# A state-space scan at the head of an eight-block kernel: weights by a second DMA queue, and half of the preparation moved into the scan

## The chip, the cores and the metric

The kernel runs on one core of a Trainium2 chip. A core has TensorE (PE, with its weight loads shown apart as PEld), VectorE (DVE), ScalarE (ACT), GpSimd (POOL) and SyncE (SP). The metric is the time on the device in microseconds (us); less is better. The time before is 2128.78 us, the median of three runs (2113.94, 2128.78 and 2228.47).

## The reference

The program sends 2048 tokens of width 128 (8 sequences of 256) through eight blocks, each as x = layernorm(x + block(x)): a state-space scan, a mixture of 8 experts, an attention with latent queries, a mixture of 64 experts, a gated linear attention, a mixture of 160 experts, six layers of linear attention, and a softmax attention. Only the first block is touched:

```python
def _L0_attn_ref(tokens, norm_w, a, b, c, skip, w_out, b_out):
    ms = jnp.mean(jnp.square(tokens), axis=-1, keepdims=True)
    x = tokens * jax.lax.rsqrt(ms + EPS) * norm_w
    x = x.reshape(B, T, H, D)                 # 8, 256, 16, 8
    a_t = jnp.tanh(a)                         # 16, 64, 64
    state0 = jnp.zeros((B, H, S), dtype=tokens.dtype)
    def step(state, x_t):
        state = jnp.tanh(jnp.einsum('bhs,hst->bht', state, a_t)
                         + jnp.einsum('bhd,hds->bhs', x_t, b))
        mixed = jnp.einsum('bhs,hsd->bhd', state, c) + skip[None] * x_t
        return (state, mixed)
    xs = jnp.moveaxis(x, 1, 0)
    _, outs = jax.lax.scan(step, state0, xs)
    outs = jnp.moveaxis(outs, 0, 1).reshape(B, T, DIM)
    return tokens + outs @ w_out.T + b_out
```

The 256 steps of the scan depend on each other; the 8 sequences and 16 heads do not.

## The kernel before

The program is straight-line code without loops at run time. A framework traces it and then orders the instructions of each engine by a simulated timeline (`schedule_with_timeline_sim=True`): the program's order is the priority, and an instruction whose operands are there in the simulation may be put ahead of one that still waits. On the chip each engine then runs its instructions in that fixed order. `behind(...)` adds an order by hand; in the scan `in_turn` gives TensorE's instructions exactly the program's order.

The 2048 tokens are held as four groups x[g] (g = 0 to 3) of 128 partitions x 4 blocks x 128 features. Group g holds sequences 2g and 2g+1; block j = 2h + m is half m of sequence 2g + h, so that half m = 0 is the first 128 tokens of a sequence. Four DMAs on SyncE's queue load them (L1269); the helper `load` (L60 to L64) puts every other load on SyncE's queue too. Its order is: the four x, three routers, `upper`, `tile_at`, two bias rows, five shared experts' weights, then in `l0_attn` (from L157) L0_a, L0_b, L0_c, L0_norm_w, L0_norm_d, L0_skip, L0_w_outT and the row L0_b_out. L0_a and L0_b have 512 KB each.

`l0_attn` prepares the scan's input group by group. POOL squares the group (L194), VectorE adds up each token's squares (L196), `inv_sqrt` takes 11 small VectorE operations (L91 to L102), four VectorE operations scale the tokens into `xs` (L200), and TensorE transposes the four blocks into one PSUM bank (`transpose4`, L128). From the bank ScalarE writes `xd` in eight operations per group (L207): the features times a column of L0_norm_d, of which a head keeps only its own features. VectorE writes `xnT` (L211), the normed input for the skip term. `xd` has the layout token pair, parity u, head-in-pair e, sequence. ScalarE also takes the tanh of L0_a (L180).

Then the scan runs in blocks of TB = 16 steps. For every eight steps, 16 products of L0_b with `xd` (L224, `inputs`) are put into two PSUM banks ahead of their use; the first of them come before the first step. A step has eight products of L0_a with the last state (L297), four for each half h of the heads, and one ScalarE tanh for each half (L306). While a half waits for its tanh, TensorE runs the other half's products, and between them two of `inputs`; after every fourth step four products of L0_c (L250, `outputs`) of the block before. When these are done, VectorE adds the skip term (L262, L263). Step 0 needs the input products of the first eight tokens of all sequences. After the scan, L336 (`xb` = 2x + b_out), the output projection (L342), L349 and a layernorm close the block, and the experts follow. L336 has no operand from the scan.

Of the kernel before, what the change touches and what calls it, by code (L numbers as in the profile page):

```python
# [10 lines left out]
F32 = mybir.dt.float32  # L11
I32 = mybir.dt.int32
U32 = mybir.dt.uint32
AF = mybir.ActivationFunctionType
ALU = mybir.AluOpType
AX = mybir.AxisListType

P = 128
B, T, D = 8, 256, 128
NT = B * T  # L20
NG = 4
# [21 lines left out]
def tile_post_ln_blocks(ctx: ExitStack, tc: tile.TileContext, I, out: bass.AP):  # L43
    nc = tc.nc
    V, S, G, PE = nc.vector, nc.scalar, nc.gpsimd, nc.tensor

    const = ctx.enter_context(tc.tile_pool(name="const", bufs=1))
    lanes = [Lane(tc, ctx, i) for i in range(2)]

    norms = [ctx.enter_context(tc.tile_pool(name=f"norm{g}", bufs=2)) for g in range(NG)]  # L50
    xs = [ctx.enter_context(tc.tile_pool(name=f"xs{g}", bufs=2)) for g in range(NG)]
    dram = ctx.enter_context(tc.tile_pool(name="dram", bufs=1, space=bass.MemoryType.DRAM))

    def bank(pool):
        return pool.tile([P, 512], F32, tag=pool.name, name=pool.name)

    def quarters(t):
        return t.rearrange("p (a b) -> p a b", b=P)

    def load(pool, key, tag=None):  # L60
        ap = I[key]
        t = pool.tile(list(ap.shape), F32, tag=tag or key, name=tag or key)
        nc.sync.dma_start(out=t, in_=ap)
        return t  # L64

    def load_row(pool, key):
# [5 lines left out]
    ident = const.tile([P, P], F32, tag="ident", name="ident")  # L72
# [10 lines left out]
    def inv_sqrt(pool, var, n, eps, scale=1.0):  # L83

        def t(tag, dt=F32):
            return pool.tile([P, n], dt, tag=f"{tag}{n}", name=tag)

        v, i, y, a, b = t("rs_v"), t("rs_i", U32), t("rs_y"), t("rs_a"), t("rs_b")  # L90
        V.tensor_scalar(v, var, scale, eps, ALU.mult, ALU.add)  # L91
        V.tensor_scalar(i, v.bitcast(U32), 1, 0xFFFFFFFF, ALU.logical_shift_right, ALU.bitwise_xor)
        V.tensor_tensor(i, i, magic[:, :n], ALU.add)
        g = i.bitcast(F32)
        V.tensor_tensor(a, g, g, ALU.mult)
        V.scalar_tensor_tensor(a, a, -1.0, v, ALU.mult, ALU.mult)
        V.tensor_scalar(b, a, 0.375, 0.875, ALU.mult, ALU.add)
        V.scalar_tensor_tensor(b, a, 1.0, b, ALU.add, ALU.mult)
        V.scalar_tensor_tensor(y, b, 1.0, g, ALU.add, ALU.mult)
        V.tensor_tensor(a, y, y, ALU.mult)  # L100
        V.scalar_tensor_tensor(a, a, -0.5, v, ALU.mult, ALU.mult)
        V.scalar_tensor_tensor(y, a, 1.5, y, ALU.add, ALU.mult)  # L102
        return y
# [20 lines left out]
    def transpose4(src, pool):  # L124

        ps = quarters(bank(pool))
        for j in range(4):
            PE.transpose(ps[:, j, :], src[:, j, :], ident)  # L128
        return ps


    x, xT = [None] * NG, [None] * NG
# [26 lines left out]
    def l0_attn(x):  # L159
# [6 lines left out]
        TB = 16  # L166
        cols = [slice(32 * c, 32 * c + 32) for c in range(4)]
        sides = [slice(0, 64), slice(64, 128)]
        with ExitStack() as es:
            wp = es.enter_context(tc.tile_pool(name="l0w", bufs=1))  # L170
            wk = es.enter_context(tc.tile_pool(name="l0k", bufs=2))
            a_sb = load(wp, "L0_a")
            b_sb = load(wp, "L0_b")
            c_sb = load(wp, "L0_c")
            normw = load(wp, "L0_norm_w")
            normd = load(wp, "L0_norm_d")
            skip = load(wp, "L0_skip")
            woT = load(wp, "L0_w_outT")
            bout = load_row(wp, "L0_b_out")
# [2 lines left out]
            xnT = wp.tile([P, T // 2, 2, B], F32, tag="xnT", name="xnT")  # L182
# [3 lines left out]
            for h in range(2):  # L186
                states.append([])
                for k in range(2):
                    t = wp.tile([P, TB * 4 * 32 + 8], F32, tag=f"st{h}{k}", name=f"st{h}{k}")
                    (V if h else G).memset(t, 0.0)  # L190
                    states[h].append(t)
            for g in range(NG):
                sq = wk.tile([P, 4, D], F32, tag="sq", name="sq")
                G.tensor_tensor(out=sq, in0=x[g], in1=x[g], op=ALU.mult)  # L194
                ms = lanes[g % 2].small.tile([P, 4], F32, tag="ms", name="ms")
                V.tensor_reduce(ms, sq, AX.X, ALU.add)  # L196
                r = inv_sqrt(norms[g], ms, 4, 1e-4, 1.0 / D)
                xs = wk.tile([P, 4, D], F32, tag="xs", name="xs")
                for j in range(4):
                    V.tensor_scalar(xs[:, j, :], x[g][:, j, :], r[:, j : j + 1], None, ALU.mult)  # L200
                ps = transpose4(xs, lanes[g % 2].ps)
                for h in range(2):
                    i = 2 * g + h
                    src = ps[:, 2 * h : 2 * h + 2, :].rearrange("p a (b u) -> p (a b) u", u=2)
                    for u in range(2):
                        for e in range(2):
                            S.activation(  # L207
                                xd[:, :, u, e, i], src[:, :, u], AF.Copy,
                                scale=normd[:, 2 * u + e : 2 * u + e + 1],
                            )  # L210
                    V.tensor_scalar(xnT[:, :, :, i], src, normw, None, ALU.mult)  # L211

            ps_m = es.enter_context(tc.tile_pool(name="ps_s", bufs=4, space=bass.MemoryType.PSUM))
            HB = TB // 2
# [69 lines left out]
            prev = [states[h][1][:, (TB - 1) * 128 :] for h in range(2)]  # L284
            for n in range(T):
                t, blk = n % TB, n // TB
                if t == 0 and blk:
                    outs, finish = outputs(blk - 1)
                if n % HB == 0:
                    now, ins = us, []  # L290
                    if n + HB < T:
                        us, ins = inputs(n + HB)
                for h in range(2):
                    for s in range(2):
                        for c in range(2):
                            k = 2 * s + c
                            in_turn(PE.matmul(  # L297
                                now[h][sides[c], n % HB // 2, n % 2, s].rearrange("p e f b -> p (e f b)"),
                                lhsT=a_sb[:, n % 2, 4 * h + k, :],
                                rhs=prev[h][:, 32 * k + 8 * (1 - c) : 32 * k + 8 * (1 - c) + 32],  # L300
                                start=False,
                                stop=(n % HB == HB - 1),
                                skip_group_check=True,
                            ))
                    st = states[h][blk % 2]
                    made_by = S.activation(  # L306
                        st[:, t * 128 : t * 128 + 128].rearrange("p (k e z b) -> p k e z b", k=4, e=2, z=2)[:, :, :, 1],
                        now[h][:, n % HB // 2, n % 2].rearrange("p s e f b -> p (s e) f b"),
                        AF.Tanh,
                    ).ins  # L310
                    if t == 0 and blk > 1:
                        tc.add_manual_dep(
                            made_by, ended[h][blk - 2].name,
                            mybir.DependencyInfo(mybir.DependencyClass.Sync, mybir.DependencyReason.DATA),
                            reason="the buffer's last block is done",
                        )
                    if t == TB - 1:
                        ended[h].append(made_by)
                    prev[h] = st[:, t * 128 : t * 128 + 136]
                    if h == 0:  # L320
                        more, ins = ins[:2], ins[2:]
                    else:
                        more, outs = (outs[:4], outs[4:]) if n % 4 == 3 else ([], outs)
                    for f in more:
                        in_turn(f())
                    if finish and not outs:
                        finish()
                        finish = None
# [129 lines left out]
    def behind(ins, other, why):  # L458

        tc.add_manual_dep(  # L460
            ins, other.name, mybir.DependencyInfo(mybir.DependencyClass.NoSync, mybir.DependencyReason.DATA), reason=why
        )
# [790 lines left out]
    with ExitStack() as moe:  # L1253
# [10 lines left out]
        x0 = []  # L1264
        with ExitStack() as es:
            xp = es.enter_context(tc.tile_pool(name="x0", bufs=NG))
            for g in range(NG):
                x0.append(xp.tile([P, 4, D], F32, tag="x0", name="x0"))
                nc.sync.dma_start(  # L1269
                    out=x0[g], in_=I["x"][g * GT : (g + 1) * GT, :].rearrange("(j p) d -> p j d", p=P)  # L1270
                )
            router0, router1, router2 = (load(mw, k) for k in ("F0_router", "F1_gate_w", "F2_router"))
            upper, tile_at = load(mw, "upper"), load(mw, "tile_at")
            bias1, bias2 = load_row(mw, "F1_gate_bias"), load_row(mw, "F2_bias")
            shared1 = tuple(load(mw, k) for k in ("F1_sg", "F1_su", "F1_sd"))
            shared2 = load(mw, "F2_sg"), load(mw, "F2_sd")
            zero = mw.tile([P, D], F32, tag="zero", name="zero")
            V.memset(zero, 0.0)
            l0_attn(x0)


        placed = [dram.tile([places, D], F32, tag=f"placed{h}", name=f"placed{h}") for h in range(2)]
# [175 lines left out]
```

## Time and profile before

| what | us |
|---|---|
| median of three runs | 2128.78 |
| lowest and highest of the three | 2113.94 and 2228.47 |
| the profiled execution's own time | 2114.01 |
| its span on the core | 2112.3 |
| preparation, up to the scan's first product (L224) | 27.03 |
| scan, up to its last step's tanh | 27.0 to 241.8 |
| PE busy over the span | 1815.5 (86%) |
| DVE, ACT, POOL busy | 1271.0, 875.4, 460.5 |
| mean granted clock of TensorE | 0.898 of full speed |

Busy time is given for each engine over the whole span; PE's is modelled, because products overlap. In a timeline row the columns are the start, the time that it covers, the engine, the line, the operation with what it writes and reads, how many instructions are merged into the row, and in brackets how long the engine had been idle and what it waited for. SPq and ACTq stand for the issue of DMAs on a queue. A row of the chain of waits has start, length, and what held the work in that time. A row of the stretches has the busy time of each engine (with the count of instructions), the granted clock, the share of the 16 DMA engines that was busy, and GB/s.

### The profile page before, as it was taken

The numbers are of one execution on the slowest core, as the hardware profiler recorded it, in microseconds if no ns is written. First come the engines' busy times: TensorE is split into PE (matmuls) and PEld (weight loads), VectorE is DVE, ScalarE is ACT, GpSimd is POOL, SyncE is SP. The second block draws the span as 40 slices with busy tenths as digits, with TensorE's granted clock in tenths as the row PEclk, the third lists the DMA queues.
The fourth block names the chain that finished last, engine by engine and source line by source line (L and its number), as shares of the span: only waits on it lengthen the run. The fifth ranks groups of instructions, "written<-read, shape, count | busy, mean of one in ns | idle before, by whom it ended". The sixth has DMA issues, their size and how long they took to land.

```text
span 2112.3 us, 38809 instructions
## 1 busy us (share of the span) xinstructions
PE 1815.5 (86%) x14138; PEld 1212.1 (57%) x14138; DVE 1271.0 (60%) x4476; ACT 875.4 (41%) x1877; POOL 460.5 (22%) x1042
## 2 busy tenths in 40 slices
PE   5999889878999999998987664679677999998797
PEld 4888645464555446544775553556455676665564
DVE  4000346867878557895559312565677998566754
ACT  4555435624754267423322111224334554434414
POOL 1000000000000000048812888850586000000000
PEclk9999989988999999998778666799888999989958
DMA  3000178403324422353147897776110000000000
GB/s 95 4 4 4 32 231 247 130 1 80 83 73 119 130 83 64 86 136 86 35 147 243 254 278 226 232 230 198 58 32 27 1 1 1 1 6 6 0 1 11
DMA packets 163455, 194.01 MB, mean 92 GB/s; under 512 B 21664, under 2 KB 117408, under 8 KB 163264
## 3 DMA queue, kind: packets, MB, share of 16 engines
q1 hardware_dynamic: 144704, 155.86, 25.5%
q0 software_dynamic: 8192, 16.79, 2.6%
q10 hardware_dynamic: 10368, 18.88, 2.4%
q8 instruction: 112, 1.84, 0.3%
q14 instruction: 79, 0.65, 0.1%
HBM read 143.68 MB, written 47.78 MB: 91 GB/s over the span
## 4 chain that ended last, share of the span: by engine, by line
PE 60%; DVE 12%; POOL 11%; DMA 7%; ACT 4%; issue 4%; SPq 2%; ACTq 0%; DVEq 0%; POOLq 0%
PE ps_s L297 7%; PE ps_o L363 6%; PE ps_m L368 6%; POOL idle L467 5%; PE ps L128 4%; PE ps_m L373 4%; POOL placed L549 4%; PE ps L1076 3%; PE ps L1070 3%; DMA w<-in_F_w_dram 3%; PE ps_o L647 3%; POOL got L658 2%; PE ps_s L224 2%; DMA got<-made,pl 2%; PE ps L1180 2%
## 5 line engine op out<-in xcount | busy, mean ns | idle before, releaser
L549 POOL DMA_INDIRECT placed<-x,pl x128 | 132.9, 1038 | 1022.5 <-DVE junk L570 915.6
L370 ACT ACTIVATE h<-ps_m 128x512 f32<-128x512 f32 x196 | 116.1, 597 | 236.8 <-PE ps_m L368 215.7
L363 PE MATMUL ps_o<-h,wd 128*128 128x512 f32 x384 | 200.8, 607 | 7.3 <-DVE h L376 7.3
L368 PE MATMUL ps_m<-xT,wg 128*128 128x512 f32 x384 | 197.7, 598 | 4.8 <-ACT h L370 4.8
L467 POOL MEMSET idle<- 128x176 f32 x768 | 192.2, 250 | 29.7
L297 PE MATMUL ps_s<-st,L_a 128*64 128x32 f32 x4096 | 192.2, 223 | 1.0
L297 PEld LDWEIGHTS ps_s<-st,L_a 128*64 128x64 f32 x4096 | 160.0, 137 | 29.6 <-ACT st L306 12.7
L376 DVE TENSOR_TENSOR h<-h,bc 128x512 f32<-128x512 f32 x192 | 131.5, 687 | 48.9 <-ACT h L370 40.2
L306 ACT ACTIVATE st<-ps_s 128x64 f32<-128x64 f32 x512 | 114.8, 224 | 99.5 <-PE ps_s L297 70.4
L658 POOL DMA_INDIRECT got<-made,pl x128 | 123.2, 962 | 111.7 <-DVE rs_v L91 86.0
L373 PE MATMUL ps_m<-xT,wu 128*128 128x512 f32 x256 | 133.9, 605 | 4.5 <-ACT h L370 3.5
L647 PE MATMUL ps_o<-w,xg 64*64 64x128 f32 x1152 | 102.5, 331 | 39.0 <-DVE xg L642 38.9
L636 PE MATMUL ps_m<-xg,w 128*64 128x64 f32 x1152 | 86.6, 266 | 54.8 <-DMA w<-in_F_w_dram 32.4
L262 DVE SCALAR_TENSOR_TENSOR outsT<-xnT,L_skip,ps 128x64 f32<-128x64 f32 x32 | 10.4, 324 | 197.4 <-PE ps L250 197.4
L363 PEld LDWEIGHTS ps_o<-h,wd 128*128 128x128 f32 x384 | 73.2, 194 | 95.8 <-issue 67.9
L368 PEld LDWEIGHTS ps_m<-xT,wg 128*128 128x128 f32 x384 | 71.2, 191 | 87.7 <-issue 65.7
L374 DVE TENSOR_TENSOR h<-h,ps_m 128x512 f32<-128x512 f32 x132 | 90.0, 682 | 44.6 <-PE ps_m L373 40.8
L636 PEld LDWEIGHTS ps_m<-xg,w 128*64 128x64 f32 x1152 | 64.1, 166 | 88.8 <-issue 33.1
L649 ACT COPY ob<-ps_o 128x512 f32<-128x512 f32 x72 | 42.1, 585 | 169.4 <-PE ps_o L647 134.0
L647 PEld LDWEIGHTS ps_o<-w,xg 64*64 64x64 f32 x1152 | 80.5, 165 | 53.9 <-DVE xg L642 46.5
L1070 PE MATMUL ps<-nT,A_w 128*128 128x512 f32 x192 | 100.3, 641 | 8.9 <-ACT nT L996 5.2
L1076 PE MATMUL ps<-A_w,hT 128*128 128x128 f32 x768 | 99.2, 282 | 7.4 <-DVE hT L1072 7.4
(357 smaller groups left out, 3718.9 us busy)
## 6 DMA issues: line engine op xcount, KB each, us to landing
bc<-comb SPq DMA_DIRECT2D x128, 256.0 KB
w<-in_F_w_dram SPq DMA_DIRECT2D x256, 96.0 KB
placed<-zero SPq DMA_DIRECT2D x72, 256.0 KB
xb<-placed SPq DMA_DIRECT2D x72, 256.0 KB
made<-ob ACTq DMA_DIRECT2D x72, 256.0 KB
w<-in_F_wg_dram SPq DMA_DIRECT2D x40, 256.0 KB
w<-in_F_wd_dram SPq DMA_DIRECT2D x40, 256.0 KB
bc<-comb SPq DMA_DIRECT2D x16, 512.0 KB
```

Source lines behind the costliest of these rows:

```text
L297: in_turn(PE.matmul(now[h][sides[c], n % HB // 2, n % 2, s].rearrange("p e f b -> p (e f b)"), lhsT=a_sb[:, n % 2, 4 * h + k, :], rhs=prev ...
L363: PE.matmul(acc[g], lhsT=w, rhs=h, start=begin, stop=end, skip_group_check=True)
L368: PE.matmul(pg, lhsT=wg, rhs=xT[g], start=True, stop=True)
L373: PE.matmul(pu, lhsT=wu, rhs=xT[g], start=True, stop=True)
L376: V.tensor_tensor(h, h, bc[:, i * GT : (i + 1) * GT], ALU.mult)
L467: after, last = G.memset(idle, 0.0).ins, after
L549: i = G.indirect_dma_start(placed[h][:, :], bass.IndirectOffsetOnAxis(rw[:, j, c : c + 1], 0), x[g][:, j, :], None).ins
L636: PE.matmul(pt[i % 2 * n : (i % 2 + 1) * n, i // 2, :], lhsT=wg[:, i, :n], rhs=xg[:, i * n : (i + 1) * n], start=True, stop=True,)
L647: PE.matmul(po[k, i // 2, :], lhsT=h[k, i // 2, :], rhs=wd[i], start=True, stop=True)
L658: i = G.indirect_dma_start(got[:, c, :], None, made[g // 2][:, :], bass.IndirectOffsetOnAxis(row[g][:, j, c : c + 1], 0)).ins
L1070: PE.matmul(ph, lhsT=w1[:, f * P : (f + 1) * P], rhs=nT, start=True, stop=True)
L1076: PE.matmul(po[:, j, :], lhsT=hT[:, f, j * P : (j + 1) * P], rhs=w2[:, f, :], start=(f == 0), stop=(f == 3),)
```

## The change

The helper `load` gets an argument for the issuing engine. L0_norm_d, L0_b and L0_a are issued by ScalarE, in this order and ahead of all other work of `l0_attn`; the other loads of the block stay on SyncE, and those of routers, biases and shared experts now follow the block in the program. `zero` is set by POOL and no longer by VectorE.

The preparation goes by halves of the sequences and no longer by groups. For half 0, ScalarE squares and adds up eight blocks (Square with an accumulator), one `inv_sqrt` works on eight columns, eight `xs` operations and eight transposes fill two banks, and `xd` is written in eight operations of 128x256, four on ScalarE and four on VectorE; `xnT` takes four of 128x256 behind them. For half 1 (`scaled(1)`), VectorE squares, sums and scales behind half 0's last `xd` operation. Its eight transposes stand in the scan, one in each of the steps 24 to 31, in TensorE's written order; after the fourth and the eighth, VectorE writes `xd` and `xnT`.

```diff
-    def load(pool, key, tag=None):
+    def load(pool, key, tag=None, by=None):
...
-        nc.sync.dma_start(out=t, in_=ap)
+        (by or nc.sync).dma_start(out=t, in_=ap)
...
-            a_sb = load(wp, "L0_a")
-            b_sb = load(wp, "L0_b")
+            normd = load(wp, "L0_norm_d", by=S)
+            b_sb = load(wp, "L0_b", by=S)
+            a_sb = load(wp, "L0_a", by=S)
+            normw = load(wp, "L0_norm_w")
             c_sb = load(wp, "L0_c")
-            normw = load(wp, "L0_norm_w")
-            normd = load(wp, "L0_norm_d")
...
-            for g in range(NG):
-                sq = wk.tile([P, 4, D], F32, tag="sq", name="sq")
-                G.tensor_tensor(out=sq, in0=x[g], in1=x[g], op=ALU.mult)
...
+            def scaled(m):
+                ms = wk.tile([P, NG, 2], F32, tag="ms", name="ms")
+                sq = wk.tile([P, D], F32, tag="sq1", name="sq")
+                for g in range(NG):
+                    for h in range(2):
+                        xj = x[g][:, 2 * h + m, :]
+                        if m == 0:
+                            S.activation(sq, xj, AF.Square, accum_out=ms[:, g, h : h + 1])
+                        else:
+                            i = V.scalar_tensor_tensor(
+                                sq, xj, 1.0, xj, ALU.mult, ALU.mult, accum_out=ms[:, g, h : h + 1]
+                            ).ins
+                            behind(i, spread[-1], "the first half of the tokens goes ahead")
+                r = inv_sqrt(wk, ms.rearrange("p g h -> p (g h)"), 2 * NG, 1e-4, 1.0 / D)
+                xs = wk.tile([P, 2 * NG, D], F32, tag="xs", name="xs")
+                for i in range(2 * NG):
+                    V.tensor_scalar(xs[:, i, :], x[i // 2][:, 2 * (i % 2) + m, :], r[:, i : i + 1], None, ALU.mult)
+                return xs
+
+            def spread_out(m, k, ps, fast):
+                ts, bs = slice(m * P // 2, (m + 1) * P // 2), slice(4 * k, 4 * k + 4)
+                src = ps.rearrange("p i (b u) -> p b u i", u=2)
+                for u in range(2):
+                    for e in range(2):
+                        scale, to = normd[:, 2 * u + e : 2 * u + e + 1], xd[:, ts, u, e, bs]
+                        if fast and e == 0:
+                            S.activation(to, src[:, :, u, :], AF.Copy, scale=scale)
+                        else:
+                            spread.append(V.tensor_scalar(to, src[:, :, u, :], scale, None, ALU.mult).ins)
+
+            def scan_norm(m, k, ps):
+                ts, bs = slice(m * P // 2, (m + 1) * P // 2), slice(4 * k, 4 * k + 4)
+                src = ps.rearrange("p i (b u) -> p b u i", u=2)
+                for u in range(2):
+                    V.tensor_scalar(xnT[:, ts, u, bs], src[:, :, u, :], normw, None, ALU.mult)
+
+            early = scaled(0)
+            halves = [transpose4(early[:, 4 * k : 4 * k + 4, :], lanes[k].ps) for k in range(2)]
+            for k in range(2):
+                spread_out(0, k, halves[k], True)
+            for k in range(2):
+                scan_norm(0, k, halves[k])
+            later = scaled(1)
...
             for n in range(T):
                 t, blk = n % TB, n // TB
+                if TB + 8 <= n < TB + 16:
+                    k, i = (n - TB - 8) // 4, n % 4
+                    if i == 0:
+                        halves[k] = quarters(bank(lanes[k].ps))
+                    in_turn(PE.transpose(halves[k][:, i, :], later[:, 4 * k + i, :], ident))
+                    if i == 3:
+                        spread_out(1, k, halves[k], False)
+                        scan_norm(1, k, halves[k])
...
+            zero = mw.tile([P, D], F32, tag="zero", name="zero")
+            G.memset(zero, 0.0)
+            l0_attn(x0)
             router0, router1, router2 = (load(mw, k) for k in ("F0_router", "F1_gate_w", "F2_router"))
...
-            zero = mw.tile([P, D], F32, tag="zero", name="zero")
-            V.memset(zero, 0.0)
-            l0_attn(x0)
```

## The prediction

> **What bounds the kernel now.** I read four views: the stretches table, the chain of waits over the first 75 us, the timeline of the same stretch, and the groups of instructions by line. The stretches come first, since they say how much there is to win.
>
> ```profile
> core 0: us, PE busy (x) PEld busy (x) DVE busy (x) ACT busy (x) POOL busy (x), PEclk, DMA share, GB/s
> 0.00:27.00 27.00, 4.69 (x16) 2.86 (x16) 20.47 (x83) 10.99 (x33) 8.47 (x13) 1.00 0.60 181
> 27.00:245.00 218.00, 215.50 (x5642) 183.73 (x5643) 18.16 (x65) 115.27 (x514) 0.00 (x0) 1.00 0.01 3
> 245.00:2112.00 1867.00, 1595.27 (x8482) 1025.51 (x8480) 1232.38 (x4328) 749.17 (x1331) 452.04 (x1029) 0.88 0.34 101
> ```
>
> TensorE does nothing but 16 transposes in the first 27 us, which is the preparation; then it is full for 218 us, which is the scan; the other 1867 us are seven further blocks, which the diff does not touch. So the front can give at most 27 us of 2112 (1.3%), and only as much of it as the scan starts earlier. The timeline says what the 27 us go into.
>
> ```profile
> 8.24 0.43 SPq L63 DMA_DIRECT2D F_sg<-in_F_sg_dram  x1
> ...
> 9.32 0.57 SPq L63 DMA_DIRECT2D L_a<-in_L_a_dram  x1
> ...
> 13.09 1.06 ACT L180 ACTIVATE L_a<-L_a 128x1024 f32<-128x1024 f32 x1 [11.06 <-DMA L_a<-in_L_a_dram]
> ...
> 15.72 2.29 ACT L207 ACTIVATE xd<-ps,L_norm_d 128x128 f32<-128x128 f32 x8 [1.58 <-DMA L_norm_d<-in_L_norm_d_dram]
> ...
> 16.80 0.69 DVE L336 SCALAR_TENSOR_TENSOR xb<-x,L_b_out 128x512 f32<-128x512 f32 x1 [1.91 <-DMA L_b_out<-in_L_b_out_dram]
> ...
> 18.98 3.32 ACT L207 ACTIVATE xd<-ps,L_norm_d 128x128 f32<-128x128 f32 x12 [0.97 <-DVE rs_y L99]
> ...
> 25.54 0.68 DVE L211 TENSOR_SCALAR xnT<-ps,L_norm_w 128x256 f32<-128x256 f32 x1 [0.34 <-ACT xd L207]
> 26.25 1.25 ACT L207 ACTIVATE xd<-ps,L_norm_d 128x128 f32<-128x128 f32 x4 [0.74 <-DVE xnT L211]
> 27.03 1.79 PEld L224 LDWEIGHTS ps_s<-xd,L_b 128*64 128x64 f32 x32 [4.20 <-ACT xd L207]
> 27.03 1.98 PE L224 MATMUL ps_s<-xd,L_b 128*64 128x64 f32 x32 [3.89 <-ACT xd L207]
> ```
>
> Two things are to be seen. First, the weights come late: SyncE's queue sends the routers and shared experts first, L_a goes out at 9.32, L_norm_d lands at 15.7, and the planner put L336, work for after the scan, where VectorE waits 1.91 us for L_b_out. Second, from 15.7 to 27.0 ScalarE and VectorE pass each PSUM bank back and forth (xd 32 x 0.286 us, xnT 8 x 0.685 us), and the scan's first product waits for the last xd. The chain of waits has the input's own part:
>
> ```profile
> 2.35 4.55 DMA x<-in_x_dram
> 6.92 0.33 SPq L63
> ...
> 27.03 1.98 PE ps_s L224 x32
> ```
>
> The last quarter of x is there at 6.9, and some load behind it on SyncE's queue waits for it. The scan is a tight loop:
>
> ```profile
> 35.90 0.66 PE L297 MATMUL ps_s<-st,L_a 128*64 128x32 f32 x16
> 36.36 0.20 PEld L224 LDWEIGHTS ps_s<-xd,L_b 128*64 128x64 f32 x4
> 36.37 0.46 ACT L306 ACTIVATE st<-ps_s 128x64 f32<-128x64 f32 x2 [0.29 <-PE ps_s L297]
> ```
>
> One step is 0.75 us (35.90 to 36.65); weight loads alone fill 0.55 + 0.20 of it, so what is put between steps on TensorE is paid.
>
> **The change, part by part.** All times are in the profiled execution: span 2112.3, time 2114.0.
>
> (1) x, a, b. L_norm_d, L_b and L_a (1 MB) are issued by ScalarE, beside the four x (1 MB) on SyncE. If the two don't disturb each other, the last x lands at 6.9 as now. If they share, 2 MB at the 318 GB/s of the stretch from 12 to 16 us, where the DMA engines were 93% busy with one queue, take 6.6 us from 2.4: 9.0. I take 9.0, the row with nearly full engines; ends 6.9 and 9.5. [...]
>
> (2) Sum of squares. POOL's 4 x 1.03 us and four reductions of 0.68 us go; in come 8 ACT Square of 128x128 with an accumulator. ACT on 128x128 costs 0.286 (2.29/8), the accumulator read 0.199 (row of L1032): 0.49 each, two per x, so 0.97 after the last x: 10.0. The Tanh of L_a (1.06 us) stands ahead of them in the program. If the planner leaves it last, 10.0; between the second and third x, 9.0 + 1.06 + 4 x 0.49 = 12.0; ahead of all, 14.0. I take 11.0, because the small x are ready before the 512 KB of L_a. ScalarE's three issues of 0.45 to 0.57 us end by 3.7 and hide behind the x.
>
> (3) inv_sqrt, once for 8 columns where there were four interleaved: 11 small operations, 0.2 us from start to start when in a row (249.04 to 250.63 holds nine): 2.2 us, 13.2. L336's two xb (0.69 each) may again be put among them, and L_b_out, now the ninth or tenth transfer, may come as late as 12; nothing to 3 us, I take 1.0: 14.2.
>
> (4) xs and transposes. Eight xs at 0.215 (0.86/4): 15.9; four transposes of the second bank at 0.28 (2.25/8): 17.0. The first bank hides under the xs.
>
> (5) Spread. 8 of 128x256, ACT and DVE alternating on each bank, second bank last: 2 x 0.384 (L641) + 2 x between 0.42 (L1016, 128x256 from PSUM) and 0.685 (L211, strided output): 1.6 to 2.1. I take 1.9, near L211, whose scattered output it resembles: 18.9. The norm for the skip term (4 x 0.685) follows behind, and has until the first block's outputs, after step 16. So the scan's first product starts at 19.0 for 27.0: **8.0 us won.**
>
> (6) The second half. `later` (8 DVE squares of some 0.46 (0.378 + 0.081, L570), 2.2 + 1.7) needs 7.6 us behind the 2.7 of (5), so it ends near 29; step 24 comes at about 40. This cover is 11 us; without it TensorE would wait. Eight transposes stand in TensorE's written order, one a step: 0.21 (two L342 within the scan moved it 0.42 us, 230.84 to 231.26) to 0.28 each, 1.7 to 2.2, and 0 if a step had slack. I take **2.0 us lost**. The 12 DVE operations behind them (12 x 0.685 = 8.2 us) are needed by step 120, 70 us later: nothing, as DVE is 92% idle in the scan; if a product had to wait for them, up to 8.2.
>
> (7) The moved loads of routers and shared experts are issued by some 18 us in both kernels and used after 245: nothing; the scan covers them. `zero` on POOL: 0.2 us beside 4.1 removed: nothing.
>
> Square and Tanh may need two tables: 1.28 us (one load at L180 now). The load would fall into the wait for x, so nothing; 1.28 for the range. [...]
>
> Sum: 2114.0 - 8.0 + 2.0 = **2108 us**. The profiled execution is beside the lowest of the three runs shown (2113.9, 2128.8, 2228.5), whose median is 0.7% higher; a median of the changed kernel may carry the same 0 to 15 us.
>
> The ends: x at 6.9, Tanh last, no xb, short spread: 6.9 + 0.97 + 2.2 + 1.7 + 1.1 + 1.6 = 14.5, so -12.5, and no cost in the scan: 2101.5. All late: 14.0 + 2.2 + 3 + 1.7 + 1.1 + 2.1 + 1.3 = 25.4, so -1.6, plus 2.2 and 8.2 in the scan: 2123.
>
> **Rivals.**
> *A, the whole front is won* (x undisturbed): about 2102. For it: the DMA engines are only 49% and 72% busy in the first 8 us. Against it: 318 GB/s is reached with one queue, and b and a go out with x.
> *B, the weights delay the input and Tanh blocks the squares*, so the scan starts near 25: -2 + 2 = 2114, no change. For it: ScalarE runs in order, and waited 11.06 us on that very Tanh.
> *C, slower: the planner's order.* The program is ordered by simulated times, which all move. Place: ScalarE's interleaving of functions. L370 alone has 45 table loads of 1.28 us among 196 activations. From 5 more switches on the path the 6 us are gone; 25 more (half again) give 2108 + 32 = 2140. Against it: all blocks behind the scan move together, so their order need not change.
> *D, the order falls out better* by as much: 2108 - 30 = 2078.
>
> **How the numbers follow.** Forecast 0.60, A 0.14, B 0.12, C 0.09, D 0.05. Two per cent, about what a measurement of this kernel can tell from no change, is 42 us, beyond everything the front holds (27); only C and D at their far ends, or the scatter of the runs (whose median stood 0.7% over the profiled time), reach it: faster 0.08, within 0.85, slower 0.07. The forecast's own range is 2101 to 2123. The range adds the 15 us between the runs shown to its upper end, 2138, and part of D below: 2090 to 2138.
>
> **What would show it.** Right: in the changed profile L224's first product near 19 and not 27; L_a and L_b landed before 10; the last x later than 6.9; in steps 24 to 31 eight gaps of 0.2 to 0.28 us and none after; the stretch behind the scan still 1867 us long. Wrong: an x later than 9.5, a VectorE wait for L_b_out above 3 us, TensorE waiting for DVE in steps 24 to 40, or a stretch behind the scan that differs by more than 10 us, which would mean that the planner, not the front, sets the result.

## The result and the profile after

The changed kernel takes 2226.2 us (median of six runs, 2216.8 to 2231.0). Beside them the kernel before ran six times: 2113.9, 2128.8, 2129.5 and 2221.4, 2228.5, 2241.5. The times of the kernel before fall into two groups some 107 us apart, and the ratio of **1.046 (95% interval 1.041 to 1.051)** sets the changed kernel against the lower one. Against that group the change made the kernel slower by 4.6%; forecast were 2108 us and no measurable change.

The profiled execution took 2222.2 us, its span is 2220.2. The first tanh of the scan and its last one cut the span into three parts (all in us):

| | first tanh | last tanh | scan | behind the scan | span |
|---|---|---|---|---|---|
| before | 29.5 | 241.6 | 212.1 | 1870.7 | 2112.3 |
| after | 21.2 | 342.4 | 321.2 | 1877.8 | 2220.2 |
| difference | -8.3 | | **+109.1** | +7.1 | +107.9 |

So the preparation became shorter by what was forecast, and the scan, whose instructions hardly changed, takes half as long again. The stretches of the changed kernel, cut at the first product, at the scan's end and at the span's end (columns as in the table of stretches shown of before):

```profile
core 0: us, PE busy (x) PEld busy (x) DVE busy (x) ACT busy (x) POOL busy (x), PEclk, DMA share, GB/s
0.00:18.00 18.00, 1.94 (x8) 1.54 (x8) 9.47 (x32) 6.65 (x21) 4.57 (x10) 1.00 0.67 201
18.00:342.00 324.00, 323.49 (x5606) 293.69 (x5608) 28.22 (x110) 115.07 (x512) 0.00 (x0) 1.00 0.02 6
342.00:2220.00 1878.00, 1599.89 (x8528) 1030.52 (x8526) 1233.60 (x4337) 749.23 (x1332) 452.70 (x1029) 0.88 0.34 100
```

TensorE is busy for the whole 324 us (323.49), so nothing makes it wait: its own instructions have become longer. ScalarE's busy time in the scan (115.07 for 512 tanh) is what it was. The granted clock still reads 1.00. Now the timeline of the changed kernel, the preparation first, then one step early in the scan:

```profile
0.74 0.43 ACTq L63 DMA_DIRECT2D L_norm_d<-in_L_norm_d_dram  x1
...
9.50 1.04 ACT L180 ACTIVATE L_a<-L_a 128x1024 f32<-128x1024 f32 x1
...
11.60 1.29 DVE L373 SCALAR_TENSOR_TENSOR xb<-x,L_b_out 128x512 f32<-128x512 f32 x2
...
15.05 1.94 PE L128 MATMUL ps<-ident,xs 128*128 128x128 f32 x8 [15.05 <-DVE xs L212]
...
18.07 1.13 PE L253 MATMUL ps_s<-xd,L_b 128*64 128x64 f32 x16 [1.08 <-DVE xd L225]
...
18.32 0.86 DVE L231 TENSOR_SCALAR xnT<-ps,L_norm_w 128x256 f32<-128x256 f32 x2
...
19.11 0.47 DVE L225 TENSOR_SCALAR xd<-ps,L_norm_d 128x256 f32<-128x256 f32 x1
...
19.64 1.12 PE L253 MATMUL ps_s<-xd,L_b 128*64 128x64 f32 x16 [0.44 <-DVE xd L225]
...
26.41 0.98 PEld L334 LDWEIGHTS ps_s<-st,L_a 128*64 128x64 f32 x16
26.51 0.22 ACT L343 ACTIVATE st<-ps_s 128x64 f32<-128x64 f32 x1 [0.20 <-PE ps_s L334]
...
27.48 0.34 PEld L334 LDWEIGHTS ps_s<-st,L_a 128*64 128x64 f32 x4
```

The first product stands at 18.07 where it stood at 27.03. But the 32 records of the sixteen input products (two for each product) now come as two pieces of 16, with a pause of 0.44 us. The second eight products read the odd tokens (u = 1), and the last `xd` operation of these, from the second bank (19.11), stands behind two `xnT` operations on VectorE. Before, all 32 came in one piece. One step lasts 1.07 us (from 26.41 to 27.48; 0.75 before), and the 16 weight loads of L_a in it alone cover 0.98 us of that. ScalarE's tanh still takes 0.22. The groups by line of the two kernels name the size; the last columns are busy time, mean ns of one, and idle time before it. Before:

```profile
L297 PE MATMUL ps_s<-st,L_a 128*64 128x32 f32 x4096 | 192.2, 223 | 1.0
L297 PEld LDWEIGHTS ps_s<-st,L_a 128*64 128x64 f32 x4096 | 160.0, 137 | 29.6 <-ACT st L306 12.7
```

After:

```profile
L334 PE MATMUL ps_s<-st,L_a 128*64 128x32 f32 x4096 | 273.5, 291 | 0.0
L334 PEld LDWEIGHTS ps_s<-st,L_a 128*64 128x64 f32 x4096 | 256.1, 225 | 23.9 <-ACT st L343 22.8
```

The same 4096 weight loads, same tile, same source, took 137 ns each and now take 225. Waits do not explain it: TensorE's idle time before these products is 0.0 us in all (1.0 before). What is left is **TensorE's own clock**, and the experiments test it. The kernel before had already shown both values, in the weight loads of its first steps:

```profile
28.69 0.55 PEld L297 LDWEIGHTS ps_s<-st,L_a 128*64 128x64 f32 x8
29.12 0.34 PEld L224 LDWEIGHTS ps_s<-xd,L_b 128*64 128x64 f32 x4
29.33 0.98 PEld L297 LDWEIGHTS ps_s<-st,L_a 128*64 128x64 f32 x16
...
30.40 0.81 PEld L297 LDWEIGHTS ps_s<-st,L_a 128*64 128x64 f32 x16
31.12 0.20 PEld L224 LDWEIGHTS ps_s<-xd,L_b 128*64 128x64 f32 x4
31.41 0.55 PEld L297 LDWEIGHTS ps_s<-st,L_a 128*64 128x64 f32 x16
```

Four weight loads of L_b go from 0.34 us to 0.20, sixteen of L_a from 0.98 over 0.81 to 0.55, between 30.4 and 31.1, some 4 us after the first product. These rows were there to be read before the prediction. In the changed kernel that step never comes in 256 steps.

### The profile page after: what moved, and what is told of

Read it like the earlier page. It is cut to its first block, busy times and chain, and to the rows that moved or that the text cites. A ratio compares the mean times of both kernels' runs of the same rounds, so it can differ in the third digit from the quotient of the medians.

```text
span 2220.2 us, 38786 instructions
## 1 busy us (share of the span) xinstructions
PE 1925.3 (87%) x14138; PEld 1325.7 (60%) x14138; DVE 1271.3 (57%) x4477; ACT 870.9 (39%) x1865; POOL 457.3 (21%) x1039
## 4 chain that ended last, share of the span: by engine, by line
PE 61%; POOL 12%; DVE 11%; DMA 7%; ACT 4%; issue 4%; SPq 2%; ACTq 0%; DVEq 0%; POOLq 0%
PE ps_s L334 10%; PE ps_o L400 6%; PE ps_m L405 6%; POOL idle L504 5%; PE ps_m L410 4%; PE ps L128 4%; POOL got L695 3%; POOL placed L586 3%; PE ps L1113 3%; PE ps_s L253 3%; DMA w<-in_F_w_dram 3%; PE ps L1107 2%; PE ps_o L684 2%; PE ps L279 2%; DMA got<-made,pl 2%
## 5 line engine op out<-in xcount | busy, mean ns | idle before, releaser
L334 PE MATMUL ps_s<-st,L_a 128*64 128x32 f32 x4096 | 273.5, 291 | 0.0
L334 PEld LDWEIGHTS ps_s<-st,L_a 128*64 128x64 f32 x4096 | 256.1, 225 | 23.9 <-ACT st L343 22.8
L253 PE MATMUL ps_s<-xd,L_b 128*64 128x64 f32 x1024 | 116.5, 330 | 1.5 <-DVE xd L225 1.5
```

Of the source, the lines that this page charges most:

```text
L253: return PE.matmul(us[h][sides[c], :, u, s, :, c, :], lhsT=b_sb[:, u, 4 * h + 2 * s + c, :], rhs=xd[:, n // 2 : (n + HB) // 2, u, :, :], s ...
L334: in_turn(PE.matmul(now[h][sides[c], n % HB // 2, n % 2, s].rearrange("p e f b -> p (e f b)"), lhsT=a_sb[:, n % 2, 4 * h + k, :], rhs=prev ...
```

## The experiments

The theory: TensorE comes out of the preparation at the lower of two clocks (0.98 us for sixteen weight loads of L_a, 0.55 at the higher); a dense stretch of products just ahead of the scan can raise it, and the scan's own small products hold it but never raise it. The change broke the stretch into two pieces. The rivals: the eight transposes inside the scan or the moved loads slow it (something in the scan itself), or the planner's order behind the scan sets the time. All extra products below write into a bank that nothing reads.

**e1_after_warm10: ten products early.** Added to the changed kernel, ahead of the preparation:

```diff
+            junk = bank(lanes[0].ps)
+            for _ in range(10):
+                PE.matmul(junk, lhsT=ident, rhs=x[0].rearrange("p a b -> p (a b)"), start=True, stop=True)
             early = scaled(0)
```

> The changed kernel with ten products of 128x128 by 128x512 in front of the preparation's transposes; their result is never read. Theory (TensorE's clock is not released at the start of the scan and stays low for all 256 steps, though the column of the granted clock says 1.00): the products run from about 4 to 14.5 us, the clock is up before the scan's first product near 18, a step takes 0.75 us instead of 1.07, weight loads of L_a 0.138 us instead of 0.225; time about 2226 - 115 = 2110. Rival (the code inside the scan is slower: the transposes in the steps, the new places of the buffers): a step stays at 1.07 us and the time at 2226.

Measured: 2247.6 us (median of four), ratio 1.062 (1.058 to 1.067); scan 321.1 us, as slow as before the edit. The timeline of TensorE shows why:

```profile
4.12 11.20 PE L236 MATMUL ps<-x,ident 128*128 128x512 f32 x20 [4.12 <-DMA x<-in_x_dram]
15.32 1.70 PE L128 MATMUL ps<-ident,xs 128*128 128x128 f32 x8
18.11 0.69 PE L258 MATMUL ps_s<-xd,L_b 128*64 128x64 f32 x16 [1.08 <-DVE xd L225]
19.67 1.12 PE L258 MATMUL ps_s<-xd,L_b 128*64 128x64 f32 x16 [0.88 <-DVE xd L225]
```

The clock did rise among the ten products (their weight loads come every 0.86 us up to 8.5 and every 0.43 from 9.1 on), and the first 16 records of the input products still ran at it: 0.69 us. Behind the second pause (0.88 us) the next 16 take 1.12. The clock was raised and lost again, ahead of the scan. In this profile the granted clock tells it too:

```profile
0.00:20.00 20.00, 13.91 (x50) 6.64 (x52) 11.44 (x37) 7.13 (x22) 4.57 (x10) 0.98 0.67 202
20.00:30.00 10.00, 10.00 (x194) 10.00 (x192) 6.21 (x37) 3.81 (x17) 0.00 (x0) 0.50 0.26 90
```

0.50 from 20 us on, for the scan whose weight loads take 225 ns, exactly as in the changed kernel, where the column says 1.00. So here the column showed a fall, and not a clock that was low from the start. As a remedy e1 failed; as a reading of the column it is the key.

**e3_after_mid: six products inside the scan**, ahead of step 128 of the changed kernel:

```diff
+                if n == 128:
+                    junk = bank(lanes[0].ps)
+                    for _ in range(6):
+                        in_turn(PE.matmul(junk, lhsT=ident, rhs=x[0]..., start=True, stop=True))
```

> The changed kernel with six products of 128x128 by 128x512 between steps 127 and 128 of the scan; their result is never read. Theory (a state of the clock, which lasts): steps before 128 take 1.07 us, from 128 on 0.75; 128 x 0.31 = 40 us and four output groups' share less, plus 7 for the products: time about 2226 - 55 + 7 = 2178. If the state doesn't last, the steps fall back to 1.07 within some us and the time is about 2233. Rival (the scan's code and buffers): steps of 1.07 on both sides, 2233.

TensorE's weight loads around them:

```profile
180.84 0.23 PEld L340 LDWEIGHTS ps_s<-st,L_a 128*64 128x64 f32 x2
...
185.31 0.34 PEld L327 LDWEIGHTS ps<-x,ident 128*128 128x128 f32 x1 [0.52 <-issue]
186.05 0.19 PEld L327 LDWEIGHTS ps<-x,ident 128*128 128x128 f32 x1 [0.41 <-issue]
...
189.14 0.31 PEld L340 LDWEIGHTS ps_s<-st,L_a 128*64 128x64 f32 x8 [0.76 <-issue]
189.37 0.20 PEld L253 LDWEIGHTS ps_s<-xd,L_b 128*64 128x64 f32 x4
```

From 181.7 on the products run at the old pace; 4.3 us later, at 186.0, a weight load falls from 0.34 to 0.19, and from 189 on every step takes 0.75 us to the end of the scan (0.20 for the four loads of L_b). The scan is 275.0 us long, 46 less than without the products, though they cost 7.5 themselves. That speaks against a slowdown by anything inside the scan: half of it, with the same work and the same moved loads, runs at the pace of before once something raised the clock. (The transposes lie in the first half, but the steps ahead of them were slow already, as the row at 26.41 shows; e6 and e7 below have the transposes and the fast pace together.) The total missed: 2216.3 us, because the stretch behind the scan grew from 1877.8 to 1922.7 us. No edit here touches that stretch, but the planner orders it anew: TensorE carries out the same 8518 instructions there, and in e3 only 63% of them stand at the same place as in the changed kernel. What in the order costs the time was not followed.

**e8_after_rest: raised, then a rest.** Three products ahead of the scan (e6 below), and eight Tanh on ScalarE that hold back the state of step 127:

```diff
+                    if n == 127:
+                        if h == 0:
+                            held = made_by
+                            for _ in range(8):
+                                r = S.activation(rest_of, a_sb..., AF.Tanh).ins
+                                behind(r, held, "a rest")
+                                held = r
+                        else:
+                            behind(made_by, held, "a rest")
```

> The changed kernel with the three products and, between steps 127 and 128, eight ScalarE operations of 128x1024 (1.06 us each, result never read) for which TensorE must wait. Theory: the clock is up to step 127 (0.75 us a step), is taken back in the 8.5 us without work, and stays low to the end of the scan (1.07 a step), since the scan alone doesn't release it: scan 214 + 8.5 + 128 x 0.32 + four more groups of outputs at the low clock, about 270 us. Rival (the start of the scan is special, as by loads or code that still arrive): the steps behind the rest are 0.75 us, scan 223 us.

TensorE's timeline around the rest, and the stretches on both sides of it:

```profile
126.61 0.78 PE L338 MATMUL ps_s<-st,L_a 128*64 128x32 f32 x16
...
128.28 0.32 PE L253 MATMUL ps_s<-xd,L_b 128*64 128x64 f32 x4
136.42 1.07 PE L338 MATMUL ps_s<-st,L_a 128*64 128x32 f32 x16 [7.82 <-ACT st L347]
137.29 0.46 PE L253 MATMUL ps_s<-xd,L_b 128*64 128x64 f32 x4
```

```profile
80.00:127.00 47.00, 46.90 (x1252) 39.83 (x1248) 3.29 (x12) 25.37 (x114) 0.00 (x0) 1.00 0.01 3
...
180.00:220.00 40.00, 40.00 (x710) 36.42 (x708) 2.20 (x8) 14.35 (x64) 0.00 (x0) 0.50 0.01 3
```

A rest of 7.82 us turned 0.75 us steps into 1.07 us steps, and they stayed so for the remaining 128 steps (1252 products in 47 us ahead of it, 710 in 40 us behind it), with the same program on both sides. The scan took 274.8 us (runs of 2226.0 and 2241.5 us). In this run the steps held the clock where it was, in both directions: high up to the rest, low for the 128 steps behind it.

**e5_before_warm3, e6_after_warm3, e7_after_warm1: products between the last transpose and the scan.** Three of them in the kernel before; three (e6) and one (e7) in the changed kernel. Their weights are the last `xs`, so that they stand behind the scaling; e5 uses `xs[:, 3, :]` for it. The edit of e7:

```diff
+            junk = bank(lanes[0].ps)
+            for _ in range(1):
+                PE.matmul(junk, lhsT=early[:, 7, :], rhs=x[0].rearrange("p a b -> p (a b)"), start=True, stop=True)
             us, todo = inputs(0)
```

> The kernel before with three products of 128x128 by 128x512 between the last transposes of the preparation and the scan's first input product; their result is never read. They need xs of the last group, so they fill TensorE's idle time from 22.7 us on. [...]

> The changed kernel with three such products between its transposes and the scan's first input product; result never read. Theory: TensorE is busy without a pause from 17 to 24 us, the scan runs at 0.75 us a step in all runs (some 214 us instead of 321); its first product comes at 20 to 22 instead of 18; time 2117, or up to 45 more by the order behind the scan. Rival (the transposes in the steps or the buffers' places slow the scan): scan of 321 us, time 2225 to 2270.

> As before, with one product instead of three. Theory: it covers 17.0 to 18.7, and the input products still have their gap near 19 to 19.6; the stretch without a pause is 2 to 3 us, so the clock is released in some runs only, or in none: a mixture of scans of 214 and 321 us, two groups of times 107 us apart. Rival (any product before the scan releases it): all runs in the lower group.

| kernel | runs | scan in the profile | behind the scan | ratio to before (95%) |
|---|---|---|---|---|
| e5 | 6, from 2143.2 to 2161.8 | 211.6 | 1904.0 | 1.013 (1.007 to 1.020) |
| e6 | 12, from 2131.7 to 2154.7 | 213.5 | 1903.0 | 1.012 (1.007 to 1.016) |
| e7 | 12, from 2103.1 to 2129.6 | 213.4 | 1875.4 | 0.997 (0.993 to 1.000) |

None of these 30 runs lies in an upper group, while of the 25 runs of the kernel before on the same chip 13 did (2215 to 2247). For e7 a mixture had been expected, and that missed: one product is enough, every time. Its timeline:

```profile
15.05 1.94 PE L128 MATMUL ps<-ident,xs 128*128 128x128 f32 x8 [15.05 <-DVE xs L212]
16.79 1.91 PE L302 MATMUL ps<-x,xs 128*128 128x512 f32 x2
18.62 1.88 PE L253 MATMUL ps_s<-xd,L_b 128*64 128x64 f32 x32
20.33 0.37 PE L337 MATMUL ps_s<-st,L_a 128*64 128x32 f32 x8
...
21.49 0.78 PE L337 MATMUL ps_s<-st,L_a 128*64 128x32 f32 x16
```

The product fills the time in which TensorE waited for `xd`, so it delays nothing that counts (first tanh 20.8, in the changed kernel 21.2), and the input products follow in one piece. TensorE works without a pause from 15.05 on, and by 20.33 the clock is up: 0.37 us for eight records, which took 0.59 us in the changed kernel. With the clock equal, the change is worth what its front is worth: first tanh 20.8 against 29.5, scan +1.3, behind the scan +4.7, hence span 2109.6 against 2112.3. In the runs that gain is not to be told from none (0.993 to 1.000). The 1.3% of e5 and e6 is the stretch behind the scan, not the scan.

**e2_before_split and e4_after_piece: the pause alone.** e2 makes the second half of the input products of the kernel before wait for the last `xnT`:

```diff
-                    V.tensor_scalar(xnT[:, :, :, i], src, normw, None, ALU.mult)
+                    normed = V.tensor_scalar(xnT[:, :, :, i], src, normw, None, ALU.mult).ins
...
+            for i, f in enumerate(todo):
+                m = f().ins
+                if i == 8:
+                    tc.add_manual_dep(m, normed.name, ...)
```

e4 makes the first input product of the changed kernel wait for all of VectorE's `xd`:

```diff
+            for i, f in enumerate(todo):
+                m = f().ins
+                if i == 0:
+                    for o in spread[:4]:
+                        tc.add_manual_dep(m, o.name, ...)
```

> The kernel before, in which the second eight of the sixteen input products ahead of step 0 wait for VectorE's last xnT, so that the burst has a gap as in the changed kernel (some 0.3 to 0.5 us). [...] Rival (the changed kernel's scan is slower in itself): no difference from the kernel before, the fast runs near 2115.

> The changed kernel in which the first input product waits for the last xd operation, so that the sixteen products before step 0 run in one piece, as in the kernel before. Theory in its narrow form (the gap of 0.44 us in this burst is what keeps the clock low): some runs near 2112 and some near 2226, as the kernel before has them near 2115 and 2228. [...] Rival (slower code): 2226 in all runs, steps of 1.07.

e2 was inconclusive as a split: the last `xnT` ended at 28.0, and the planner had put the product that waits for it in thirteenth place of the sixteen, at 28.1, so no pause came about. Its six runs fall into the two groups as those of before do (2119 and 2128; 2220 to 2240; ratio 1.002, 0.996 to 1.008). But its profile caught one of the upper group, with the front of before:

```profile
26.84 1.97 PE L224 MATMUL ps_s<-xd,L_b 128*64 128x64 f32 x32 [3.89 <-ACT xd L207]
...
35.64 1.01 PE L303 MATMUL ps_s<-st,L_a 128*64 128x32 f32 x16
```

The input products come in one piece as in the kernel before (1.97 us there and here 1.98), and yet a group of a step's products still takes 1.01 us nine microseconds later, where the row shown of before (35.90) has 0.66. The scan took 317.0 us. So the **upper group of the kernel before is the scan at half clock** (weight loads of L_a of 226 ns in e2, and of 225 in e1, where the column reads 0.50), as far as e2 and e9 below show it (a profile of the unedited kernel from that group was not taken), and with one unbroken burst of 2 us ahead of the scan the clock rises in about half of the runs: 27 of the 53 runs of the kernel before shown in this study are in the lower group.

e4 did what it was to do:

```profile
19.75 1.98 PE L253 MATMUL ps_s<-xd,L_b 128*64 128x64 f32 x32 [2.65 <-DVE xd L225]
```

One piece again, although TensorE now waits 2.65 us for it; and a lower group came back, 3 of 6 runs (2151.1, 2152.8, 2155.1 against 2258.8, 2261.3, 2275.6; ratio of the lower ones 1.016, 1.012 to 1.021). The profiled run is an upper one, with a scan of 321.1 us; that the lower ones are the fast scan is read from their times alone. Another 38 us lie behind the scan (1915.9 against 1877.8 in the changed kernel), as in e3.

**e9_loads_only, e10_prep_only: the change in two.** e9 is the kernel before with the loads of the changed one (ScalarE's queue, the new order of loads, `zero` on POOL); e10 is the changed kernel with the loads of before:

```diff
-            normd = load(wp, "L0_norm_d", by=S)
-            b_sb = load(wp, "L0_b", by=S)
-            a_sb = load(wp, "L0_a", by=S)
+            a_sb = load(wp, "L0_a")
+            b_sb = load(wp, "L0_b")
...
+            normd = load(wp, "L0_norm_d")
```

> The kernel before with only the first part of the change: L_norm_d, L_b and L_a issued by ScalarE, routers and shared experts behind the block. Theory: the front gets shorter by the late weights alone (L_norm_d was there at 15.7 and L_b_out at 16.8; the xd and xnT operations, 11.3 us, stay), so the first input product comes at some 22 to 25 instead of 27.0; the sixteen products stay in one piece, so there are two groups of runs as before, with scans of 212 and 321 us. Rival (the second queue's weights are what spoils the scan): all runs in the upper group, near 2220.

> The changed kernel with all loads on SyncE's queue in the old order, so only the halved preparation and the transposes within the scan. Theory: the front waits for the late weights (L_norm_d near 15.7), the first input product comes at 19 to 21; the input products come in two pieces if xnT stands ahead of the last xd again, and then all runs are in the upper group, near 2225. If they come without a pause, two groups 107 us apart. Rival: a scan at 0.75 us a step in all runs.

e9: 2099.3 once, and 2214.2 to 2215.9 three times. Its profile is one of the upper three:

```profile
25.09 1.97 PE L224 MATMUL ps_s<-xd,L_b 128*64 128x64 f32 x32 [3.45 <-ACT xd L207]
...
28.57 1.01 PE L297 MATMUL ps_s<-st,L_a 128*64 128x32 f32 x16
```

The first product stands at 25.09 in one piece, so the loads alone bring 1.9 us, and both groups are still there. The scan takes 317.2 us without a transpose in it, with 1.01 us for a group of a step's products, as in e2. e10: 2212.7 to 2231.9, four of four in the upper group, ratio 1.050 (1.042 to 1.057), with the pause:

```profile
18.26 1.12 PE L253 MATMUL ps_s<-xd,L_b 128*64 128x64 f32 x16 [5.97 <-DVE xd L225]
20.07 1.12 PE L253 MATMUL ps_s<-xd,L_b 128*64 128x64 f32 x16 [0.68 <-DVE xd L225]
```

The new preparation brings nearly all of the gain in the front (first tanh 21.7) and, by these runs, does the harm, whatever queue the weights take. Four runs are few: with a chance of a half, four of four come in 6% of cases. For the changed kernel itself e12 makes the count firmer.

**e11_tight: e7 with the front tightened.** On top of e7, the tanh of L_a stands behind the squares, and `xb` and `xnT` stand behind the `xd` that the scan waits for:

```diff
-            S.activation(a_sb, a_sb, AF.Tanh)
...
+                if m == 0:
+                    behind(S.activation(a_sb, a_sb, AF.Tanh).ins, squared, "the tokens first")
...
+                    if m == 0:
+                        behind(i, spread[3], "the scan's input first")
...
+                behind(i, spread[3], "the scan's input first")
```

> The changed kernel with the one product ahead of the scan that kept all runs at the high clock, and with three things out of the way of the front: the Tanh of L_a behind the last Square (1.04 us), xb behind the last xd (1.29 us), xnT behind the last xd (0.78 us). Theory: the first input product comes at some 16 instead of 18.6, the scan takes 213 us in all runs, the time is 2112 - 3 = 2109 if the order behind the scan stays, up to 45 more if not. Rival (a shorter front leaves the product too short again): runs of 2220 among them.

Measured: 2112.5 us (six runs, 2100.5 to 2121.7, none in an upper group), ratio 0.998 (0.991 to 1.004):

```profile
13.07 1.94 PE L128 MATMUL ps<-ident,xs 128*128 128x128 f32 x8 [13.07 <-DVE xs L213]
14.80 1.91 PE L305 MATMUL ps<-x,xs 128*128 128x512 f32 x2
16.64 1.21 PE L256 MATMUL ps_s<-xd,L_b 128*64 128x64 f32 x32
```

The transposes came 2.0 us earlier and the input products ran at full clock almost from the start (1.21 us for 32, 1.88 in e7); the first tanh is at 18.2, 2.6 us ahead of e7's. In the runs that is not to be told apart from e7.

**e12_after_again: the changed kernel, unedited, once more** on that chip:

> The changed kernel itself once more, on another chip. Theory in its narrow form (with the gap in its input products the clock is never released): all runs near 2225. Theory in its wide form (chance, as with the kernel before, in which about half of the runs are low): some runs near 2115.

Measured: 2205.6 to 2227.8 in six runs, ratio 1.046 (1.039 to 1.052), scan 321.1 us. Together with the first six that is none of twelve in the lower group; of the kernel before it is 27 of 53. The stretch behind the scan took 1861.4 us here and 1877.8 in the first profile, with the same program in the same order, so a difference of up to 16 us there, such as the 7.1 and 4.7 above, says nothing of an edit.

## Why the prediction was wrong

**Where it was right: the front, in part by luck.** The third x landed at 8.7 and the fourth at 9.55, as the semaphore of its transfer in the trace shows (before: 6.90; taken: 9.0, upper end 9.5). So the last x came 2.6 us later once the weights moved beside it, close to the case of term (1) in which the two share. The Tanh fell between the squares of the third and the fourth x (9.50), a place that term (2) does not list; there it held the fourth x's squares back from 9.6 to 10.45, and the squares ended at 11.3 (taken: 11.0, a value between two listed cases). `xb` stood inside `inv_sqrt` for 1.29 us (taken: 1.0), the transposes ended at 17.0 (17.0). Term (5), 8.0 us won, measured 8.3 by the first tanh. What it missed was an order: `xnT` ahead of the last `xd`, which ended at 19.6 (taken: 18.9).

**Term (6), the transposes, was sized at the wrong clock.** In steps of the changed kernel with a transpose the step is 1.62 us instead of 1.07, so 0.55 each and 4.4 for eight; that fits the 4.2 us by which its scan (321.2) exceeds the half-clock scan of e2 (317.0). At full clock, in e7, the scan is 1.3 us longer than that of before for eight transposes, under the 2.0 taken. The second half was ready in time; TensorE is busy throughout, as was said.

**The step that failed stands ahead of the sum:** "The scan is a tight loop" with "One step is 0.75 us", read from steps at 36 us and taken as a property of the instructions. It is a property of the clock at that moment. Of the 107.9 us between the two profiled spans, the scan makes 109.1. The sum had no term for it, the stated range ended 88 us below the result, and no rival had it: C, the slower one, named the planner's order and more table loads; the stretch behind the scan, its place, gave 7.1 us and has 99 table loads in both profiles, so it is not the cause.

**Two rows had shown it.** The run at 2228.5 among three was read as "the scatter of the runs". It lay 100 us above the other two, which lay 15 apart, and asked for a cause: by e2 and e9, the same scan at half clock, as the changed kernel had it in both profiles and, by the times, in all twelve runs. And the weight loads at 28.7 to 31.4, shown above, change from 0.98 to 0.55 with no edit between them. The granted clock in the table of stretches could not have warned: it reads 1.00 for the scan at either pace, before and after.

**Against the upper group of before the change is no loss.** The 26 upper runs of before have a median of 2228.1, the changed kernel 2226.2 and 2210.9: no slower at equal clock, as far as runs on several chips can say. What the change lost is the chance of the high clock, half of 107 us in a mean, and all of it in a comparison with the lower group.

**What stays open.** That the two pieces keep the clock low rests on e4 (3 of 6 against 0 of 12; if both had the same chance, a split as uneven as this would come in 2 of 100 cases) and on the extra product of e7 (12 of 12), which also lengthens the work. e4 moves the first product from 18.07 to 19.75 as well, and no run has the later start without the single piece. Nor do the runs separate the length of the pause from the length of the pieces. Why the scan's products, with TensorE busy without a gap, hold a high clock but do not raise a low one was not taken apart. The 66 us between the shortest and the longest stretch behind the scan (1861.4 in e12, 1927.4 in e8) were not followed through the planner either.

## What to carry to other kernels

Before a step's time is taken as given, compare the mean of one and the same instruction between the start, the middle and the end of its stretch: a weight load that takes 137 ns here and 225 there points to the clock, and the number of runs in each group of times says how often. An edit that shortens the way to a chain of small products should be checked for the run-up that it leaves: here a dense, unbroken one of 4.6 to 6.2 us (e5, e6, e7 and e11) left none of 36 runs in an upper group, and one of 2.0 us (the kernel before) left 26 of 53 there. One product of 128x512 put into a wait that was there anyway cost nothing and was worth 108 us of scan against the changed kernel (213.4 to 321.2 in the profiles). Of the versions run, e7 and e11 are the ones to keep: against the lower group of before they are level (0.997 and 0.998), and over all runs e7's mean is 2113.2 against 2175.0 for the kernel before on the same chip, because all twelve of its runs come out low.

## What the runs showed of the hardware

- TensorE came to the scan's input products at the low pace in the kernel before, the changed kernel, e2, e4, e9 and e10 (16 records in 1.12 or 1.13 us, 32 in 1.97 or 1.98; 16 took 0.69 in e1 at the high pace), and to the extra products in e1 and e3. The low pace can last: 321 us in the changed kernel, with TensorE busy throughout. The pace doubles within one row (0.86 us between two products of 128x512 to 0.43, e1 and e3).
- It had risen 5.0 us (e1) and 4.3 us (e3) after the first dense product, about 4 in the kernel before. In e6, e7 and e11 the transposes come straight ahead of the product. Counted from their start it had risen after 3.4 us in e6 (weight load of 0.20 us at 19.14), by 5.3 in e7 (20.33) and, as an estimate, after 3.7 in e11 (32 weight loads of L_b in 1.07 us from 16.64 on; 1.01 in e6, all of them fast); counted from the product after 1.7, by 3.5 and after 2.0. What sets the moment, and why a burst of about 2 us succeeds in half of the runs of the kernel before, was not shown. Busy time alone did not raise it: TensorE shows as busy for 323.49 of 324 us in the changed kernel, and the clock stays low.
- The high clock was lost within a short time in e1: between 18.8 and 19.7 us, although none of TensorE's pauses since its first product was longer than 1.08 us.
- The low clock, once it is not left at the start, costs 109 us of 2112 here, 5%.
- The granted clock of a stretch read 1.00 for a scan at the low pace wherever the profile held no fall (the changed kernel, e2, e4), and 0.50 for the same pace where it did (e1, e8). The duration of the weight loads of L_a told the paces apart: a mean of 225 or 226 ns in scans that are low throughout (the changed kernel, e1, e2, e4), 136 or 137 in the others (before, e5, e6, e7), and 181 where the pace changed on the way (e3, e8).
